# The square roots of the queries' norms, moved on the scalar engine of a decoder layer

## The chip, the core and the metric

The kernel runs on one core of a Trainium2 chip, on one NeuronCore with five engines that work side by side: TensorE (matrix products, here "PE", with "PEld" for loading its weights), VectorE ("DVE"), ScalarE ("ACT"), GpSimd ("POOL") and SyncE ("SP", which here only starts transfers). The metric is the device time of one execution in microseconds (us). The kernel before took 1009.03 us, the median of three runs (1007.69 to 1009.83).

## What is computed

A decoder layer on x of 16 x 64 x 512: self attention along one axis, cross attention to a context, and a mixture of 16 experts of which each row takes 4. The change lies in the cross attention, cut here to what matters:

```
q = (hidden @ Wq.T)  -> 32 heads of 128;   k, v -> 8 heads of 128, each used by 4 query heads
q = q * rsqrt(mean(q*q) + 1e-5) * q_norm_w          # one root for each row and head
k = k * rsqrt(mean(k*k) + 1e-5) * k_norm_w
probs = softmax(q @ k.T / sqrt(128) + mask)          # exponentials
out = (probs @ v) @ Wo.T
```

Everything is float32. The queries' norm needs a square root, the softmax an exponential. On this chip both are functions of ScalarE, and they lie in different tables: each change from one to the other shows in the trace as an instruction of its own, ACT_TABLE_LOAD. Squares and copies need no such load in this trace.

## The kernel before

The rows stand in 8 tiles of 128, taken in pairs u = 0 to 3. A head group g = 0 to 7 is one key head with its four query heads. One **step** (g, u) is one head group and one pair. `cross` runs over the steps, first g = 0 to 3 and then 4 and 5, with u inside; for the last two head groups it runs over u with (6, u) and (7, u) inside. So there are 32 steps. Around a step's own attention it does other work:

- `step_queries` (L492) normalises the queries of the step: `normed_queries` multiplies each half by its reciprocal root (L480, VectorE), turns it on TensorE (L483) and copies it out of PSUM times the weight (L489 on ScalarE or L487 on VectorE). L497 ties the two halves together.
- `attended` (L553) of the step before multiplies the turned probabilities by the values (L559) and copies the result, `at`, out (L565, ScalarE); `left_sums` (L229 to L232) makes sums of it on GpSimd, or on VectorE for the last two head groups.
- `softmaxed` (L500) makes the scores (L509), takes them out of PSUM with the mask (L514), then the maximum (L528), the difference (L529), the exponential (L530, ScalarE), the sum (L531), its reciprocal (L539) and the product (L540). For g of 6 and 7 eight shorter exponentials take the place of one (L536). L522 multiplies the next step's reciprocal roots by a one that is made from this step's scores: it changes no value and only makes them wait for the scores.
- `queries` (L447) makes the raw queries of the step three ahead, or of (7, u) in step (6, u): 28 matrix products (`seven`, L255, Strassen's scheme in Winograd's form), sums on VectorE (L459 to L463), and eight squares with their sums on ScalarE (L467). After some of them `inverse_root` takes the root (L443) and its reciprocal (L444, VectorE): for head groups 1 to 6 once for two pairs, after u = 1 and u = 3, for the last head group after every pair.
- `projected` (L573) multiplies the attention's result of the step before by Wo, again in 28 products (L255), with its sums on VectorE (L580 to L587). `right_sums` (L236 to L239) prepares the weights of a head group on GpSimd when a new one begins.
- `turned_rows` (L543) turns the probabilities (L546, TensorE) and copies them out of PSUM as `pt` (L550, ScalarE). `pt` is read by the next `attended`; its PSUM bank is one of two that all transposes share.

In the last two head groups `summed`, `normed_pair` (with a root of its own, through the same L443) and `routed_pair` follow, which prepare the experts' part. L823 enters rows into tables with indirect transfers from GpSimd.

The order on each engine is not written out by hand. It comes from the program's builder, which takes the text's order as a priority. So the order in the trace differs from the text's at places: L458, a copy that `queries` starts with, runs ahead of the exponential of `softmaxed`, which stands before it in the text.

Of the kernel before, what the change touches and what calls it, by code (L numbers as in the profile page):

```python
# [23 lines left out]
F32 = mybir.dt.float32  # L24
I32 = mybir.dt.int32
AF = mybir.ActivationFunctionType
ALU = mybir.AluOpType
AX = mybir.AxisListType

P = 128  # L30
N, C, L = 16, 64, 512
NT = N * C // P
DC = L // P
KVH, GRP, HD = 8, 4, 128
# [5 lines left out]
EPS = 1e-5  # L40
# [9 lines left out]
def decoder_layer(  # L50
# [25 lines left out]
    V, S, T, G = nc.vector, nc.scalar, nc.tensor, nc.gpsimd  # L76
# [3 lines left out]
    small = ctx.enter_context(tc.tile_pool(name="small", bufs=4))  # L80
# [13 lines left out]
    def tr_bank():  # L94
        return bank("tr", 2)

    def sc_bank():
        return bank("sc", 3)
# [90 lines left out]
    eps_sb = const.tile([P, 1], F32, tag="eps", name="eps_sb")  # L189
# [44 lines left out]
    def right_sums(engine, t, w):  # L234
        b11, b12, b21, b22 = (w[:, 2 * k : 2 * k + 2, 256 * n : 256 * n + 256] for k in range(2) for n in range(2))
        engine.tensor_sub(t[:, 0], b12, b11)  # L236
        engine.tensor_sub(t[:, 1], b22, t[:, 0])  # L237
        engine.tensor_sub(t[:, 2], b21, t[:, 1])  # L238
        engine.tensor_sub(b12, b22, b12)  # L239

    def seven(a11, a12, d, a22, s, t, w, sums_last=False):

        b11, t3, b21, b22 = (w[:, 2 * k : 2 * k + 2, 256 * n : 256 * n + 256] for k in range(2) for n in range(2))
        x, p, r = (mm_bank().rearrange("p (a n) -> p a n", a=2) for _ in range(3))
        p7 = sc_bank()[:, :256]
        products = [
            (x[:, 0], a11, b11), (x[:, 1], s[:, 1], t[:, 1]), (p7, d, t3),
            (p[:, 0], a12, b21), (p[:, 1], s[:, 2], b22),
            (r[:, 0], a22, t[:, 2]), (r[:, 1], s[:, 0], t[:, 0]),
        ]  # L250
        if sums_last:
            products = [products[k] for k in (0, 3, 5, 6, 1, 2, 4)]
        for dst, left, right in products:
            for k in range(2):
                T.matmul(dst, left[:, k, :], right[:, k, :], start=k == 0, stop=k == 1)  # L255
        return x, p7, p, r
# [173 lines left out]
    q_raw, q_ss, q_rs = {}, {}, {}  # L430
# [7 lines left out]
        left_sums(V, s, *xn_quarters(u))  # L438
        xn_sums.append(s)

    def inverse_root(x, shape, scale):
        rs = small.tile(shape, F32, tag="rs{}".format(len(shape) * shape[1]), name="rs", bufs=2)
        S.activation(rs, x, AF.Sqrt, bias=eps_sb, scale=scale)  # L443
        V.reciprocal(rs, rs)  # L444
        return rs

    def queries(g, u):  # L447
        w = wq_tiles[g]
        if u == 0:
            q_ss[g] = small.tile([P, NT, GRP], F32, tag="qss", name="qss", bufs=2)  # L450
            if g > 0:
                right_sums(G, wq_t, w)
        raws = [work.tile([P, GRP, HD], F32, tag="qraw", name="qraw", bufs=8) for _ in range(2)]
        c1, c2 = (raw.rearrange("p (a h) d -> p a (h d)", a=2) for raw in raws)
        x, p7, p, r = seven(*xn_quarters(u), xn_sums[u], wq_t, w, sums_last=(g, u) == (0, 0))
        su = work.tile([P, 2, 256], F32, tag="su", name="su", bufs=1)
        u3 = work.tile([P, 256], F32, tag="u3", name="u3", bufs=1)
        S.copy(su[:, 0], x[:, 0])  # L458
        V.tensor_add(su[:, 1], x[:, 1], su[:, 0])  # L459
        V.tensor_add(u3, p7, su[:, 1])  # L460
        V.tensor_add(c1, p, su)  # L461
        V.tensor_add(c2, r, u3.unsqueeze(1).to_broadcast([P, 2, 256]))
        V.tensor_add(c1[:, 1], r[:, 1], c1[:, 1])  # L463
        for j, raw in enumerate(raws):
            for h in range(GRP):
                square = work.tile([P, HD], F32, tag="square", name="square", bufs=1)
                S.activation(square, raw[:, h, :], AF.Square, accum_out=q_ss[g][:, 2 * u + j, h : h + 1])  # L467
            q_raw[g, 2 * u + j] = raw

        done = (0, 1, 2, 3) if g == KVH - 1 else (0, 1, 3) if g == 0 else (1, 3)  # L470
        if u in done:
            first = max([k + 1 for k in done if k < u], default=0)
            span = 2 * (u + 1 - first)
            rs = inverse_root(q_ss[g][:, 2 * first : 2 * u + 2, :], [P, span, GRP], 1.0 / HD)
            for k in range(first, u + 1):
                q_rs[g, k] = rs[:, 2 * (k - first) : 2 * (k - first) + 2, :]

    def normed_queries(g, i, on_vector):
        raw = q_raw.pop((g, i))
# [20 lines left out]
    def softmaxed(g, u, qts):  # L500
        sp = sc_bank()
        for hp in range(2):
            for b in range(2):
                for j, qt in enumerate(qts):
                    k0 = (2 * u + j) * P + b * C
                    at = ((j * 2 + hp) * 2 + b) * C

                    for h in range(2):
                        T.matmul(  # L509
                            sp[h * C : (h + 1) * C, at : at + C], qt[:, b, 2 * hp + h, :],  # L510
                            kT[g // 4][:, g % 4, k0 : k0 + C], start=True, stop=True,
                        )
        pr = work.tile([P, 8, C], F32, tag="prob", name="prob")
        V.scalar_tensor_tensor(  # L514
            pr, sp.rearrange("p (a k) -> p a k", a=8), HD**-0.5,
            mask_sb.unsqueeze(1).to_broadcast([P, 8, C]), ALU.mult, ALU.add,
        )
        after = divmod(NT // 2 * g + u + 1, NT // 2)
        if after[0] < KVH - 2:

            rs = q_rs[after]
            V.scalar_tensor_tensor(  # L522
                rs, pr[:, 0:1, 0:1].to_broadcast([P, 2, GRP]), HIGHEST, rs, ALU.is_le, ALU.mult
            )
        mx = small.tile([P, 8], F32, tag="mx", name="mx")
        sm = small.tile([P, 8], F32, tag="sm", name="sm")
        if g < KVH - 2:
            V.tensor_reduce(mx, pr, AX.X, ALU.max)  # L528
            V.tensor_sub(pr, pr, mx.unsqueeze(2).to_broadcast([P, 8, C]))  # L529
            S.activation(pr, pr, AF.Exp)  # L530
            V.tensor_reduce(sm, pr, AX.X, ALU.add)  # L531
        else:

            V.tensor_reduce(mx, pr, AX.X, ALU.max, negate=True)
            for a in range(8):
                S.activation(  # L536
                    pr[:, a, :], pr[:, a, :], AF.Exp, bias=mx[:, a : a + 1], accum_out=sm[:, a : a + 1]
                )
        V.reciprocal(sm, sm)  # L539
        V.tensor_mul(pr, pr, sm.unsqueeze(2).to_broadcast([P, 8, C]))  # L540
        return pr

    def turned_rows(pr):  # L543
        tp = tr_bank()
        for a in range(4):
            T.transpose(  # L546
                tp[:, a * P : (a + 1) * P], pr[:, 2 * a : 2 * a + 2, :], ident
            )
        pt = work.tile([P, 2, 2 * P], F32, tag="pt", name="pt", bufs=1)
        S.copy(pt.rearrange("p j t -> p (j t)"), tp)  # L550
        return pt
# [59 lines left out]
    def cross(steps):  # L611
        mixing = None
        for g, u in steps:
            if u == 1 and g + 2 < KVH:
                load_wq(g + 2)
            if u == 0 and g + 1 < KVH:
                load_wo(g + 1)
            qts = step_queries(g, u)
            if mixing:
                late.append((*mixing[:2], *attended(*mixing)))  # L620
                mixing = None
            pr = softmaxed(g, u, qts)
            if g < KVH - 2:
                queries(*divmod(NT // 2 * g + u + 3, NT // 2))
            elif g == KVH - 2:
                queries(g + 1, u)
            if (g, u) == (KVH - 3, NT // 2 - 1):
                queries(g + 1, u)
            if late:
                projected(*late.pop())  # L630
            if (g, u) == (KVH - 1, NT // 2 - 1):
                shared_hidden(0, 0, mm_bank)
            pt = turned_rows(pr)
            if g < KVH - 2 and (g, u) != steps[-1]:

                mixing = (g, u, pt)
            else:
                late.append((g, u, *attended(g, u, pt)))
            if g == KVH - 2 and u > 0:
                summed(u - 1)  # L640
                normed_pair(u - 1)
                if u > 1:
                    entered(u - 2, 1)
            if g == KVH - 1 and u > 0:
                routed_pair(u - 1)
                entered(u - 1, 0)
            if (g, u) == (KVH - 2, 0):
                load_shared(0)
            if (g, u) == (KVH - 2, NT // 2 - 1):
                load_shared(1)  # L650
# [483 lines left out]
```

## Time and profile before

| | |
|---|---|
| median of three runs | 1009.03 us (1007.69 to 1009.83) |
| the profiled execution | 1009.14 us, of which the profile's span is 1007.4 us |
| ACT_TABLE_LOAD | 18 at L443, 13 at L530, 5 at L536, each 1283 ns |
| roots of queries (L443) | 13 of 128x16 (307 ns), 6 of 128x8 (301 ns) |
| squares (L467) | 256 of 309 ns, each with a read of its sum of 187 ns |
| exponentials | 24 of 630 ns (L530), 64 of 334 ns (L536) |
| steps of the cross attention | from 192 to 730 us of the span |
| granted TensorE clock over the span | 0.990 |

How to read it: times in a view are microseconds from the start of the span. "A <- B" in a list of waits means that engine and instruction A stood idle until B was done. In the order of time each line gives the start, the length, the engine, the source line, and what is written from what; a bracket at the end gives the idle time before it and what ended it. A line of stretches gives the busy time of PE, PEld, DVE, ACT and POOL (each with a count of instructions), then the clock that TensorE was granted as a share of the full one, then the share of the DMA engines and GB/s.

### The profile page before, as it was taken

The numbers are of one execution on the slowest core, as the hardware profiler recorded it, in microseconds if no ns is written. First come the engines' busy times: TensorE is split into PE (matmuls) and PEld (weight loads), VectorE is DVE, ScalarE is ACT, GpSimd is POOL, SyncE is SP. The second block draws the span as 40 slices with busy tenths as digits, with TensorE's granted clock in tenths as the row PEclk, the third lists the DMA queues.
The fourth block names the chain that finished last, engine by engine and source line by source line (L and its number), as shares of the span: only waits on it lengthen the run. The fifth ranks groups of instructions, "written<-read, shape, count | busy, mean of one in ns | idle before, by whom it ended". The sixth has DMA issues, their size and how long they took to land. (4 is left out here: it accounts for less than half of the span.)

```text
span 1007.4 us, 14841 instructions
## 1 busy us (share of the span) xinstructions
PE 956.2 (95%) x5080; PEld 662.8 (66%) x5080; DVE 552.4 (55%) x1188; ACT 445.0 (44%) x1260; POOL 336.3 (33%) x356
## 2 busy tenths in 40 slices
PE   9999998999999999999999999988999999999994
PEld 4456555888888888887888877766754445445442
DVE  3665657876767677667767667668475111111110
ACT  2366672655454554435544675564530222222221
POOL 2131102341614427135243241033053344454433
PEclk9999999999999999999999999998999999999997
DMA  9220014200201102012020110000033966655763
GB/s 231 75 95 21 11 32 108 102 1 1 84 1 42 43 1 85 1 60 77 1 85 1 43 43 1 23 22 22 22 104 131 353 156 150 153 107 127 190 174 72
DMA packets 28960, 76.88 MB, mean 76 GB/s; under 512 B 4624, under 2 KB 9024, under 8 KB 26832
## 3 DMA queue, kind: packets, MB, share of 16 engines
q1 hardware_dynamic: 18160, 52.96, 15.8%
q0 software_dynamic: 10432, 22.66, 11.0%
q8 instruction: 42, 0.69, 0.3%
q14 instruction: 38, 0.31, 0.1%
q10 hardware_dynamic: 288, 0.26, 0.1%
HBM read 102.31 MB, written 14.97 MB: 116 GB/s over the span
## 5 line engine op out<-in xcount | busy, mean ns | idle before, releaser
L997 PE MATMUL sc<-w,xt 128*128 128x512 f32 x288 | 130.3, 593 | 2.3 <-DMA w<-in_wu_dram 2.3
L467 ACT ACTIVATE square<-qraw 128x128 f32<-128x128 f32 x256 | 79.2, 309 | 85.0 <-DVE qraw L461 42.1
L997 PEld LDWEIGHTS sc<-w,xt 128*128 128x128 f32 x288 | 51.8, 190 | 54.1 <-issue 52.4
L229 POOL TENSOR_TENSOR sat<-at 128x256 f32<-128x256 f32 x24 | 17.5, 728 | 202.2 <-ACT at L565 202.2
L1002 DVE TENSOR_TENSOR z<-sc,z 128x256 f32<-128x256 f32 x36 | 15.3, 425 | 124.8 <-ACT z L1001 118.9
L255 PE MATMUL mm<-wo_sb,at 128*128 128x256 f32 x256 | 68.8, 394 | 5.4 <-ACT at L565 5.4
L255 PE MATMUL mm<-wq_sb,xnT 128*128 128x256 f32 x256 | 72.5, 389 | 0.0
L1025 POOL DMA_INDIRECT out_dram<-y,idx x36 | 57.3, 1593 | 36.9 <-DMA out_dram<-y,idx 30.4
L1017 PE MATMUL mm<-w,zt 128*128 128x512 f32 x144 | 68.0, 594 | 1.5 <-DVE zt L1010 1.5
L255 PE MATMUL mm<-wq_t,xns 128*128 128x256 f32 x256 | 66.2, 381 | 2.6 <-POOL wq_t L237 1.5
L255 PE MATMUL mm<-wo_t,sat 128*128 128x256 f32 x256 | 67.3, 383 | 0.6 <-DVE sat L230 0.6
L979 POOL DMA_INDIRECT xg<-rows_d,idx x40 | 39.7, 993 | 75.3 <-PE tr L1008 50.5
L823 POOL DMA_INDIRECT table_d<-entry_sb,at_slot x24 | 25.6, 1065 | 111.6 <-DVE at_slot L790 105.2
L1001 ACT ACTIVATE z<-sc 128x256 f32<-128x256 f32 x36 | 13.8, 384 | 106.9 <-PE sc L997 106.9
L255 PEld LDWEIGHTS mm<-wo_sb,at 128*128 128x128 f32 x256 | 49.6, 196 | 14.4 <-ACT at L565 7.6
L255 PEld LDWEIGHTS mm<-wq_t,xns 128*128 128x128 f32 x256 | 48.3, 190 | 9.8 <-POOL wq_t L237 1.9
L255 PEld LDWEIGHTS mm<-wo_t,sat 128*128 128x128 f32 x256 | 48.7, 193 | 7.8 <-POOL wo_t L238 0.7
L1017 PEld LDWEIGHTS mm<-w,zt 128*128 128x128 f32 x144 | 27.1, 190 | 35.3 <-issue 32.1
L565 ACT COPY at<-sc 128x512 f32<-128x512 f32 x64 | 34.3, 588 | 35.3 <-PE sc L559 35.0
L480 DVE TENSOR_TENSOR qraw<-qraw,rs 128x512 f32<-128x512 f32 x64 | 48.2, 757 | 0.2
L255 PEld LDWEIGHTS mm<-wq_sb,xnT 128*128 128x128 f32 x256 | 44.3, 190 | 5.7 <-DVE su L459 0.3
L467 ACT ACTIVATION_READ_ACCUMULATOR square<-qraw 128x1 f32 x256 | 47.8, 187 | 0.0
(286 smaller groups left out, 2082.5 us busy)
## 6 DMA issues: line engine op xcount, KB each, us to landing
w<-in_wg_dram SPq DMA_DIRECT2D x40, 512.0 KB
w<-in_wu_dram SPq DMA_DIRECT2D x40, 512.0 KB
w<-in_wd_dram SPq DMA_DIRECT2D x40, 512.0 KB
wq_sb<-in_wq_dram SPq DMA_DIRECT2D x8, 1024.0 KB
wo_sb<-in_wo_dram SPq DMA_DIRECT2D x8, 1024.0 KB
xs<-in_x_dram SPq DMA_DIRECT2D x8, 256.0 KB
wv_sb<-in_wv_dram SPq DMA_DIRECT2D x2, 1024.0 KB
ct<-in_ctxt_dram SPq DMA_DIRECT2D x8, 256.0 KB
```

Of the source, the lines that this page charges most:

```text
L229: engine.tensor_add(s[:, 0], a21, a22)
L255: T.matmul(dst, left[:, k, :], right[:, k, :], start=k == 0, stop=k == 1)
L467: S.activation(square, raw[:, h, :], AF.Square, accum_out=q_ss[g][:, 2 * u + j, h : h + 1])
L480: V.tensor_mul(raw, raw, q_rs[g, i // 2][:, i % 2, :].unsqueeze(2).to_broadcast([P, GRP, HD]))
L565: S.copy(at[:, :, b * C : (b + 1) * C], pv[b].rearrange("p (a q) -> p a q", a=2 * GRP))
L823: G.indirect_dma_start(tables_d[q], bass.IndirectOffsetOnAxis(at_slots[u][:, q : q + 1], axis=0), entry_sb[:, 2 * u + j, k, :], None,)
L979: G.indirect_dma_start(xg, None, rows_d, bass.IndirectOffsetOnAxis(idx[:, b : b + 1], axis=0))
L997: T.matmul(hp, xt[:, d, :], w1_tiles[buffer(j)][:, :, d, :], start=(d == 0), stop=(d == DC - 1))
L1001: S.activation(z, hp[:, :FI], AF.Silu)
L1002: V.tensor_mul(z, hp[:, FI:], z)
L1017: T.matmul(op, zt[:, c, :], w2_tiles[buffer(j)][:, c, :], start=(c == 0), stop=(c == FI // P - 1))
L1025: G.indirect_dma_start(out, bass.IndirectOffsetOnAxis(idx[:, b : b + 1], axis=0), y, None, bounds_check=NT * P - 1, oob_is_err=False, comp ...
```

## The change

Only the place of the queries' roots changes. `queries` no longer takes them at its end, except for the first two pairs of head group 0, which are needed before the first step; it puts the task into a list, `waiting`. A new function, `query_roots`, does what stood there. It is called at two places:

- in `softmaxed` of the next step, right behind the exponential. This takes the roots of all head groups but the last.
- in `cross`, right behind `turned_rows` of the same step, for the last head group.

At both places the root's bias, the constant 1e-5, is made anew by a small instruction on VectorE from one column of the tile that the exponential, or the copy of `pt`, has just written: the minimum with 0 and then the maximum with 1e-5. Its value is always 1e-5, but the root can't start before that tile is written. The tie L522 is left out in the steps at which the next step's roots are not yet taken.

```diff
-    def inverse_root(x, shape, scale):
+    def inverse_root(x, shape, scale, eps=eps_sb):
...
-        S.activation(rs, x, AF.Sqrt, bias=eps_sb, scale=scale)
+        S.activation(rs, x, AF.Sqrt, bias=eps, scale=scale)
...
         if u in done:
             first = max([k + 1 for k in done if k < u], default=0)
-            span = 2 * (u + 1 - first)
-            rs = inverse_root(q_ss[g][:, 2 * first : 2 * u + 2, :], [P, span, GRP], 1.0 / HD)
-            for k in range(first, u + 1):
-                q_rs[g, k] = rs[:, 2 * (k - first) : 2 * (k - first) + 2, :]
+            if g == 0 and u < NT // 2 - 1:
+                query_roots(g, first, u)
+            else:
+                waiting.append((g, first, u))
+
+    waiting = []
+
+    def query_roots(g, first, u, after=None):
+        eps = eps_sb
+        if after is not None:
+
+            eps = small.tile([P, 1], F32, tag="eps", name="eps", bufs=1)
+            V.tensor_scalar(eps, after, 0.0, EPS, ALU.min, ALU.max)
+        span = 2 * (u + 1 - first)
+        rs = inverse_root(q_ss[g][:, 2 * first : 2 * u + 2, :], [P, span, GRP], 1.0 / HD, eps)
+        for k in range(first, u + 1):
+            q_rs[g, k] = rs[:, 2 * (k - first) : 2 * (k - first) + 2, :]
...
-        if after[0] < KVH - 2:
+        if after in q_rs and after[0] < KVH - 2:
...
+        while waiting:
+            query_roots(*waiting.pop(), after=pr[:, 0, 0:1])
         V.reciprocal(sm, sm)
...
             pt = turned_rows(pr)
+            if waiting and waiting[0][0] == KVH - 1:
+                query_roots(*waiting.pop(), after=pt[:, 0, 0:1])
```

## The prediction

> **What bounds the kernel.** I read the page's first part, then the list of waits for TensorE alone, then the order of time on each engine around every root (L443), then the granted clock in short stretches.
>
> ```profile
> PE 956.2 (95%) x5080; PEld 662.8 (66%) x5080; DVE 552.4 (55%) x1188; ACT 445.0 (44%) x1260; POOL 336.3 (33%) x356
> ...
> PE sc L509 <- DVE qt L497: 5.6, 7, 1.4
> PE mm L255 <- ACT at L565: 5.4, 7, 1.2
> PE sc L559 <- ACT pt L550: 4.8, 3, 2.1
> PE tr L483 <- ACT pt L550: 2.6, 5, 1.4
> ```
>
> TensorE is the bound, so the change can win only what TensorE waits for. The first line is the page's, the others are the four longest of TensorE's waits (us in total, times, longest): 18.4 us, all in the attention steps. I number the 32 steps (g,u) in order of execution; 24 to 31 are (6,0), (7,0), (6,1), (7,1) and so on. From one L509 to the next, most steps of heads 1 to 5 take 15.90 us with TensorE never idle: with a root or without one, nothing can be won there. The stalls sit in steps 1, 4, 8, 12, 16, 20, 22 and 24 to 30.
>
> In step 28 the order of time (start, length) on ScalarE, then on TensorE, and a row of the stretches read:
>
> ```profile
> 661.50 1.28 ACT L443 ACT_TABLE_LOAD   x1
> 662.79 0.30 ACT L443 ACTIVATE rs<-qss,eps_sb 128x8 f32<-128x8 f32 x1
> 663.00 0.56 ACT L550 COPY pt<-tr 128x512 f32<-128x512 f32 x1
> 664.78 1.07 ACT L565 COPY at<-sc 128x512 f32<-128x512 f32 x2 [1.22 <-PE sc L559]
> ...
> 663.62 1.14 PE L559 MATMUL sc<-pt,v 64*128 64x256 f32 x8 [2.06 <-ACT pt L550]
> ...
> 666.00:667.00 1.00, 1.00 (x3) 0.82 (x4) 1.00 (x5) 0.05 (x1) 0.99 (x1) 0.50 0.03 1
> ```
>
> The load and the root stand ahead of pt, whose transposes ended at 661.55; TensorE waits 2.06 us, then 1.16 us for `at`. After that its granted clock (third number from the right) is 0.50 from 666.0 to 669.4. Step 30 is the same (2.06, 1.16, half clock from 700.1 to 706.9).
>
> **The change, part by part.**
>
> *Counts.* All 23 roots stay (19 of queries, 4 of L668). Of 18 loads for the root and 13 for L530 one each goes, as steps 23 and 24 no longer switch twice. Of 23 ties (L522, 240 ns) 11 go; 17 `eps` instructions on VectorE come, a 128x1 tensor_scalar, which the rows of L720 and L723 give at 0.15 us: 2.6 us out, 2.6 in. No DMA is moved, and nothing passes SP's or POOL's queue.
>
> *The new place, heads 0 to 5.* The load needs no operand, so it runs right behind the exponential; the root then needs `eps`. In step 4 the exponential and what follows it on ScalarE:
>
> ```profile
> 255.93 0.63 ACT L530 ACTIVATE prob<-prob 128x512 f32<-128x512 f32 x1 [1.43 <-DVE prob L529]
> 258.72 0.31 ACT L467 ACTIVATE square<-qraw 128x128 f32<-128x128 f32 x1 [2.16 <-DVE qraw L461]
> ```
>
> Load and root are 1.28 + 0.31 = 1.59 us; the gap behind an exponential without a load before it is 2.16 us, so they are covered. The load back (1.28) falls before the next step's exponential, as now, in its 1.43. Behind the root wait the squares on ScalarE, then on VectorE the reciprocal and two L480, which the transposes need only some 7 us later. If the cover were gone, squares would move pt, which waits 1.34 us on its own in step 5: a slip under that costs nothing. Cost taken: 0; bounds 0 and 0.5 us in each of 12 steps (VectorE holding L463 beyond the 1.76 us that it ends ahead of the product needing its bank: 277.81 against 279.57).
>
> *Step 1.* The load at 205.23 holds the `at` copies; TensorE's 0.42 goes: **-0.4**.
>
> *Steps 4, 8, 12, 20.* pt is 0.50 us late, TensorE waits 0.29; then L497 takes 0.81 instead of 0.18 us and the next scores wait (step 4, POOL and VectorE):
>
> ```profile
> 267.10 1.27 POOL L239 TENSOR_TENSOR wo_sb<-wo_sb 128x512 f32<-128x512 f32 x1
> 267.59 0.81 DVE L497 SCALAR_TENSOR_TENSOR qt<-qt 128x8 f32<-128x8 f32 x1
> ```
>
> L497 is held until POOL's L239 is nearly over. With pt on time, L497 would start 2.82 us behind L546's start, as in step 6 (281.30 to 284.12): at 267.10, the very hundredth in which L239 starts. Ahead of it, the step is 15.90 instead of 17.02: 1.1 us won; behind it, it ends where it does now: 0. Among near ties of 0.01 or 0.02 us in this trace (L522 against L230) VectorE lost two and won two. Half: 4 x 1.1 / 2, **-2.2** (0 to -4.4).
>
> *Step 16.* pt could start at 459.70, not 461.31. L483 then comes 1.55 us earlier, L497 at 461.92 ends with POOL's L237 near 462.2 instead of 464.62; of that 2.4 I take **-2.0** (-1.4 to -2.4).
>
> *Step 22.* The reciprocal of head group 6, which has no tie, lets four L480 (2.65 us) in ahead of L487 and L497; the step is 17.21. These move behind step 23's exponential, where VectorE idles 0.8 to 1.1 us three times: **-1.3** (0 to -1.3).
>
> *Steps 24 and 25.* The roots of (6,2) and (6,3) come behind eight exponentials: squares 1.6 us later, ending at 597.0, still ahead of pt (598.26). But the root of (7,0) comes behind pt, so its first L480 goes from 597.35 to about 600, among POOL's eight operations of right_sums, and each operation that alternates with them waits up to 1.3 us. TensorE's 0.36 before the projection becomes 1.2, and the sums of `at` finish later: **+1.5** (0 to +3).
>
> *Step 26.* pt was on time; now load and root (to 629.1) hold the `at` copies, 628.80 before: **+0.3**.
>
> *Steps 28 and 30.* pt starts at 661.56, L559 at 662.2; its `at` copies could start 1.16 later, but load and root end at 663.64. The projection starts at 664.76, not 665.90: -1.1. With 0.67 + 1.5 us of stalls around 1.13 of work, instead of 2.06 + 1.16, half clock becomes unlikely: in step 26 (0.68 + 1.16) it stayed at 1.00. Half clock for 3.4 us costs 1.7 us; VectorE, busy without a break from 656 to 667.7, lets 1.3 of it through: **-2.4** (0 to -2.8). Step 30 gains more, as L559 itself took 2.08 at half clock: -1.1 and -1.9, **-3.0** (0 to -3.6).
>
> The halving in rows comes with gaps of 2.06 us at most. [...]
>
> The load's row is 1.28 us and the root starts 1.29 behind it (263.91, 265.20). [...]
>
> **Sum.** -0.4 - 2.2 - 2.0 - 1.3 + 1.5 + 0.3 - 2.4 - 3.0 = -9.5. The profiled execution took 1009.14 (span 1007.4 and 1.74 around it), 0.11 above the median of the runs. Forecast: **999.6 us**. It reaches the end because the stages behind stay TensorE's (711 to 770: busy 57.16 of 59).
>
> **Rivals.**
> - *Half clock stays* in 28 and 30, as the new stall of 1.5 us keeps the stretch thin: +3.2, 1002.8. For it: 1.13 of work in 3.3 us. Against it: step 26.
> - *The gain is eaten in heads 0 to 5*: VectorE takes `eps`, then waits for the root in order, and L461 to L463 slip past their 1.76 us: 12 x 0.6 = +7.2, 1006.8. For it: VectorE waits up to 2.1 us for a root today (L444). Against it: the engines' order already differs with and without a load, so the load is reckoned with in it.
> - *Slower: the queries of (7,u) become the wait.* Behind pt now stand load, root, reciprocal, L480, transposes, L489: 1.28 + 0.31 + 0.2 + 0.69 + 0.65 + 0.69 = 3.8, less 1.13 of L559: 2.7 us for each of four steps, if TensorE has the transposes L483 ahead of the projection. +10.7, against the gains outside of 24 to 30 (5.9) and half a stall: about 1013. It decides once more than two of the four steps are so ordered. For it: step 24 has that order. Against it: in 26, 28 and 30 L483 comes some 8 us behind L559.
>
> **Chances.** Forecast 0.55 (its own range 996 to 1003), half clock 0.17, eaten 0.15, slower 0.13. A measurement of this kernel tells about 0.2% (2 us) from no change. Faster: 0.55 + 0.17 + half of the third = 0.79; same 0.10; slower 0.11. The range reaches from all ties won and little lost in 24, 995.5, to the third case, 1007.
>
> **What would show it.** Loads of L443 17, of L530 12; the load right behind L530 in steps 1, 3, ... 23; "L559 <- pt" and "L483 <- pt" nearly gone from TensorE's waits; L497 at 0.18 in about half of steps 4, 8, 12, 20; clock 1.00 through steps 28 and 30; step 25 longer. Wrong if the written order isn't kept on the engines: already L458 runs ahead of the exponential that the text puts before it.

## The result, and the profile after

The changed kernel takes **1002.1 us** (median of four runs, 1000.3 to 1002.5) against 1009.0: a ratio of 0.993, 95% interval 0.991 to 0.995. The forecast was 999.6 with a range of 995.5 to 1007.0. The gain is 6.9 us where 9.5 were expected. The profiled execution took 1002.03 us, with a span of 1000.3.

TensorE's row of the page and its longest waits in the attention steps after the change (L487, L497, L509, L546, L550, L559 and L565 are now L500, L510, L522, L561, L565, L574 and L580; L480 and L483 are L493 and L496):

```profile
PE 953.4 (95%) x5080; PEld 661.5 (66%) x5080; DVE 549.3 (55%) x1194; ACT 441.7 (44%) x1258; POOL 334.7 (33%) x356
```

```profile
PE mm L255 <- ACT at L580: 5.9, 6, 1.4
PE sc L522 <- DVE qt L510: 4.3, 5, 1.2
...
PE sc L574 <- ACT pt L565: 2.0, 3, 0.7
...
PE tr L496 <- DVE qraw L493: 1.7, 2, 1.0
```

Of the two waits for `pt` (4.8 and 2.6 us) 2.0 are left. The wait for `at` has grown by 0.5 us, the one for the tie has shrunk by 1.3 us, and one is new: transposes that wait for the queries of the last head group (L493). The loads stand as counted, in the groups of ScalarE by line (busy us, ns of one, then its idle time before):

```profile
L443 ACT ACT_TABLE_LOAD x17 | 21.8, 1283 | 10.3 <-DVE eps L485 10.2
L543 ACT ACT_TABLE_LOAD x12 | 15.4, 1283 | 0.2
```

The 10.2 us of idle time in the first line are no part of the forecast. In step 9 the exponential, the load and the root read:

```profile
334.49 0.63 ACT L543 ACTIVATE prob<-prob 128x512 f32<-128x512 f32 x1 [0.84 <-DVE prob L542]
336.05 1.28 ACT L443 ACT_TABLE_LOAD   x1 [0.93 <-DVE eps L485]
337.35 0.31 ACT L443 ACTIVATE rs<-qss,eps 128x16 f32<-128x16 f32 x1
```

The load did not run right behind the exponential but stood 0.93 us until `eps` was written, and so in eleven of the twelve steps (3, 5, ... 23). In steps 26, 28 and 30 it starts 0.02 us behind the copy of `pt`, as was forecast.

The difference by steps, each from its first scores to the next step's, the last one to the first product of the shared expert (L868 before, L885 after):

| steps | before, us | after, us | difference | forecast |
|---|---|---|---|---|
| 1 | 13.77 | 13.31 | -0.46 | -0.4 |
| 4, 8, 12, 20 | 68.06 | 66.92 | -1.14 | -2.2 |
| 16 | 17.29 | 14.86 | -2.43 | -2.0 |
| 22 | 17.21 | 15.89 | -1.32 | -1.3 |
| 24 and 25 | 30.47 | 34.01 | +3.54 | +1.5 |
| 26 and 27 | 36.39 | 36.39 | 0.00 | +0.3 |
| 28 and 29 | 37.05 | 34.69 | -2.36 | -2.4 |
| 30 and 31 | 26.58 | 23.28 | -3.30 | -3.0 |

All other steps are equal to 0.02 us. The sum is -7.47. The steps also begin 0.99 us earlier (192.45, 191.46), ahead of anything that was changed, and what follows them takes 1.33 us more: from 717.97 to 721.38, shortly behind the last L574, the clock is halved, and the last product with the gate (L753) ends 1.69 us later behind the shared expert's first one than before. That makes 7.1 us of span.

So two terms missed, the ties and steps 24 and 25. Step 24 on TensorE (start, length; the bracket is the idle time before and what ended it), and the stretches around it (busy PE, PEld, DVE, ACT, POOL, then the granted clock):

```profile
591.54 0.60 PE L561 MATMUL tr<-ident,prob 128*128 128x128 f32 x4
592.82 1.14 PE L574 MATMUL sc<-pt,v 64*128 64x256 f32 x8 [0.67 <-ACT pt L565]
595.00 1.07 PE L496 MATMUL tr<-ident,qraw 128*128 128x128 f32 x4 [1.04 <-DVE qraw L493]
596.76 1.09 PE L496 MATMUL tr<-ident,qraw 128*128 128x128 f32 x4 [0.70 <-DVE qraw L493]
```

```profile
591.60:595.00 3.40, 1.68 (x14) 1.00 (x12) 2.60 (x6) 1.85 (x4) 3.13 (x3) 1.00 0.71 289
595.20:598.40 3.20, 2.50 (x10) 1.71 (x9) 3.17 (x3) 1.20 (x2) 3.20 (x3) 0.50 0.00 0
598.60:601.80 3.20, 3.20 (x35) 2.38 (x34) 3.20 (x3) 1.27 (x1) 3.12 (x3) 0.50 0.00 0
```

The four transposes take 1.07 instead of 0.66 us: TensorE ran at half clock here for 6.8 us, which it did not before. In steps 28 and 30 the half clock of before is gone.

### The profile page after: what moved, and what is told of

Its sections match the earlier page's. It is cut to its first block, busy times and chain, and to the rows that moved or that the text cites. A ratio compares the mean times of both kernels' runs of the same rounds, so it can differ in the third digit from the quotient of the medians.

```text
span 1000.3 us, 14858 instructions
## 1 busy us (share of the span) xinstructions
PE 953.4 (95%) x5080; PEld 661.5 (66%) x5080; DVE 549.3 (55%) x1194; ACT 441.7 (44%) x1258; POOL 334.7 (33%) x356
## 5 line engine op out<-in xcount | busy, mean ns | idle before, releaser
L467 ACT ACTIVATE square<-qraw 128x128 f32<-128x128 f32 x256 | 79.0, 308 | 65.7 <-DVE qraw L463 38.7
L580 ACT COPY at<-sc 128x512 f32<-128x512 f32 x64 | 34.3, 587 | 31.7 <-PE sc L574 31.4
L493 DVE TENSOR_TENSOR qraw<-qraw,rs 128x512 f32<-128x512 f32 x64 | 47.8, 753 | 0.5
L467 ACT ACTIVATION_READ_ACCUMULATOR square<-qraw 128x1 f32 x256 | 47.7, 186 | 0.0
```

The source lines that it names most:

```text
L493: V.tensor_mul(raw, raw, q_rs[g, i // 2][:, i % 2, :].unsqueeze(2).to_broadcast([P, GRP, HD]))
L580: S.copy(at[:, :, b * C : (b + 1) * C], pv[b].rearrange("p (a q) -> p a q", a=2 * GRP))
```

## The experiments

Theory: the parts of the change act one by one, and each term of the table has the cause that the prediction named. Rivals: the two misses come from another part of the change than was thought, or the half clock follows something else than TensorE's idle time. The lengths of steps below are read from each run's trace; the medians stand beside the kernel before on the same chip, which took 1009.2 to 1009.8 us there.

**The two halves apart.** The roots of the last head group back in the queries:

```diff
-            if g == 0 and u < NT // 2 - 1:
+            if (g == 0 and u < NT // 2 - 1) or g == KVH - 1:
```

> The changed kernel, but the roots of head group 7 are taken in the queries again, ahead of the copy of the turned probabilities; the roots of heads 1 to 6 stay behind the exponential. My theory: the two halves of the change add up. Steps 1, 4, 16 and 22 keep what they gained (0.5 + 1.1 + 2.4 + 1.3 = 5.3 us), steps 24 and 25 take 30.5 us again instead of 34.0, and steps 28 and 30 fall back to their old lengths, half clock included (37.05 for 28 and 29, 22.5 for 30): 1009.0 - 5.3 = 1003.7 us. Rival: the loss in steps 24 and 25 comes from the roots of (6,2) and (6,3), which stand behind the eight exponentials here too, so they stay at 34.0 us and the time is 1007.2.

Measured: 1006.7 us, ratio 0.997 (0.995 to 0.999), 3 us above the expectation. Steps 1, 16 and 22 kept their gains to 0.02 us. Step 4 lost its tie here (17.01), so all four ties were lost. Steps 24 and 25 took 31.17 us: neither number of the expectation, but most of the loss is gone, and 0.70 us stay with the exponential's half. Steps 28 and 29 took 37.69, 30 and 31 28.12, each with one more stretch of half clock than before.

The other half alone:

```diff
-            if g == 0 and u < NT // 2 - 1:
+            if g < KVH - 1:
```

> The kernel before, but with the roots of head group 7 behind the copy of the turned probabilities; heads 0 to 6 as before. My theory: steps 28 and 30 gain 2.4 + 2.0, steps 24 and 25 lose 3.5, and nothing else moves: 1009.0 - 0.9 = 1008.1 us. Rival (steps 24 and 25 lose only by both halves together): they lose 0 to 1 us here and the time is 1004.6 to 1005.6.

Measured: 1010.9 us, ratio 0.9995 (0.997 to 1.002): nothing won. Steps 28 and 29 (34.70) and 30 and 31 (23.28) are those of the changed kernel, but steps 24 and 25 took 36.73 us, worse than in both cases expected. The load is not shared with the roots of (6,2) and (6,3) any more, so it stands between `pt` and the root, and TensorE waits 2.27 us for L493, with 10.2 us of half clock behind it. The two halves help each other here.

**The root of (7,0) alone**, ahead of `pt` again:

```diff
-            if g == 0 and u < NT // 2 - 1:
+            if (g == 0 and u < NT // 2 - 1) or (g, u) == (KVH - 1, 0):
```

> The changed kernel, but the root of (7,0), the first of the last head group, is taken in the queries, ahead of the copy of the turned probabilities; those of (7,1) to (7,3) stay behind it. My theory: the 3.5 us lost in steps 24 and 25 come from this one root being late, so that its L493 meet POOL's sums and the clock is halved. Here steps 24 and 25 take 30.5 us (30.2 to 31.0), the clock is 1.00 in them, and the time is 1002.1 - 3.5 = 998.6 us. Rival: another part of the change (the squares 1.6 us later, the roots of (6,2) and (6,3) behind eight exponentials) is the cause: 33 to 34 us for the two steps, 1001.1 to 1002.1 in all.

Measured: 1000.8 us, ratio 0.991 (0.990 to 0.993); steps 24 and 25 take 31.16 us at a clock of 1.00 (30.2 to 31.0 were expected, and 998.6 us in all). So 2.85 of the 3.54 us belong to this one root, as the theory has it. The other 0.70 are in the first experiment too. VectorE's order in step 24 of this run:

```profile
592.44 0.68 DVE L493 TENSOR_TENSOR qraw<-qraw,rs 128x512 f32<-128x512 f32 x1
593.04 0.20 DVE L444 RECIPROCAL rs<-rs 128x8 f32<-128x8 f32 x1
593.15 0.69 DVE L602 TENSOR_TENSOR acc<-mm,acc 128x512 f32<-128x512 f32 x1
593.76 2.93 DVE L493 TENSOR_TENSOR qraw<-qraw,rs 128x512 f32<-128x512 f32 x2
```

The first line is the last of four L493 of (6,2) and (6,3), whose roots now come behind step 24's exponentials; before, all four (L480) ran from 581.17 to 584.27, ahead of step 24. Now they fill VectorE until the reciprocal that (7,0) needs, and TensorE takes L574 first and waits 0.68 us for `pt`, where before it had a transpose of (7,0) to do. The last line shows that the two L493 of (7,0) meet POOL's sums in this run too: 2.93 us, where the two L480 took 0.69 and 1.16 before, and TensorE waits 0.89 us for the second. That the order and this meeting make the 0.70 us is read from the trace; no run tried either by itself.

**Clock or wait.** Two runs fill stalls of TensorE with matmuls whose results nobody reads, without making anything else earlier. In the kernel before, five of them ahead of L559 in steps 28 and 30:

```diff
         pv = [sc_bank() for _ in range(2)]
+        for _ in range(5 if g == KVH - 2 and u >= 2 else 0):
+            T.matmul(
+                pv[0][:, :256], v[g // 4][:C, 2 * u, g % 4 * HD : (g % 4 + 1) * HD],
+                last["pr"][:C, :4, :], start=True, stop=True,
+            )
```

> The kernel before, with five matmuls of 64x256 more in steps 28 and 30, between the transposes of the probabilities and L559, written to the bank that L559 then overwrites; they need nothing that L559 waits for, and fill 1.4 of TensorE's 2.06 us there. All else is unchanged, the late copy too. My theory: the clock goes by the idle share of a fixed stretch of 3.41 us (in the traces so far it fell behind stretches with 1.72 us of idle time or more and stayed at 1.00 up to 1.69), so it stays at 1.00 in steps 28 and 30; 28 and 29 take some 35.8 instead of 37.05 us, step 30 some 20.6 to 21 instead of 22.46, and the time is 1009.0 - 3 = 1006 us. Rival: the clock answers to something else (the load of the root's table, VectorE being busy): half clock as before, 1009.

Measured: 1005.0 us, ratio 0.995 (0.993 to 0.996). The stretches of step 28 in this run:

```profile
659.00:662.00 3.00, 2.37 (x13) 1.69 (x12) 3.00 (x9) 2.86 (x11) 2.39 (x3) 1.00 0.02 1
662.00:665.50 3.50, 2.34 (x16) 1.68 (x15) 3.50 (x9) 2.24 (x6) 2.58 (x4) 1.00 0.01 1
665.50:669.00 3.50, 3.50 (x19) 2.91 (x20) 2.32 (x8) 1.80 (x3) 2.09 (x2) 1.00 0.07 18
```

`pt` is as late as before (2.07 us behind the transposes), the load is where it was, and the clock stays at 1.00. Steps 28 and 29 take 35.43 us, 30 and 31 24.23. The half clock's price is thus 1.62 and 2.35 us; the change's earlier `pt` adds 0.74 and 0.95 to that (to 34.69 and 23.28).

In the changed kernel, step 24 alone, two ahead of L574 as above and three behind it, which read `pt` and write to a bank of the transposes:

```diff
+        if (g, u) == (KVH - 2, 0):
+            spare = tr_bank()
+            for _ in range(3):
+                T.matmul(
+                    spare[:, :256], v[g // 4][:C, 2 * u, g % 4 * HD : (g % 4 + 1) * HD], pt[:C, 0, :],
+                    start=True, stop=True,
+                )
```

> The changed kernel, with five matmuls of 64x256 more in step 24 alone: two between the transposes of the probabilities and L574 (0.56 us in a stall of 0.67), three behind L574 (0.84 us in a stall of 1.04), results unused. My theory: of the 2.85 us that the late root of (7,0) costs in steps 24 and 25 (34.01 against 31.17 with the root early), the larger part is half clock, 6.8 us of it. With the stalls filled the clock stays at 1.00 and the two steps take 32.0 us (31.7 to 32.6); the time is 1002.1 - 2 = 1000 us. Rival: the loss is the late L493 and their meeting with POOL alone, the half clock runs beside VectorE's sums: 33.5 to 34.2 us for the two steps, 1002 in all.

Measured: steps 24 and 25 take 32.48 us at full clock, so 1.53 us of the loss were half clock. The time is 1001.9 us, ratio 0.992 (0.990 to 0.994), and not 1000: in this execution half clock fell into step 30 instead (24.75 against 23.28 us). That led to a count of all traces (last section).

**The tie.** Steps 8, 12 and 20 of the changed kernel are still long, for one hundredth of a microsecond. VectorE in step 4, which was won, and in step 8, then POOL in the same two:

```profile
265.66 0.18 DVE L510 SCALAR_TENSOR_TENSOR qt<-qt 128x8 f32<-128x8 f32 x1
...
329.25 1.28 DVE L510 SCALAR_TENSOR_TENSOR qt<-qt 128x8 f32<-128x8 f32 x1
```

```profile
265.67 1.32 POOL L239 TENSOR_TENSOR wo_sb<-wo_sb 128x512 f32<-128x512 f32 x1
...
329.24 1.26 POOL L239 TENSOR_TENSOR wo_sb<-wo_sb 128x512 f32<-128x512 f32 x1
```

In step 4 the tie starts 0.01 us ahead of L239 and takes 0.18 us, in step 8 it starts 0.01 behind and takes 1.28. The edit makes the tie read its first operand from the bank of PSUM (`turned`, which `normed_queries` returns as well) that the second tile is copied from:

```diff
-            first, second = (qt[:, :, :, 0:1] for qt in qts)
+            first = qts[0][0][:, :, :, 0:1]
+            second = qts[1][1].rearrange("p h b q -> p b h q")[:, :, :, 0:1]
             V.scalar_tensor_tensor(first, second, HIGHEST, first, ALU.is_le, ALU.mult)
```

> The changed kernel, but the tie of the two query tiles (L510, 128x8) reads its first operand from the bank of PSUM that the second tile was copied from, not from the second tile in SBUF; same size, same wait, same place. My theory: in steps 8, 12 and 20 the tie is held by POOL's L239 since both read two operands from SBUF; with one operand in PSUM it takes 0.25 us or less beside POOL, those steps take 15.90 instead of 17.01 us, and the time is 1002.1 - 3.3 = 998.8 us (step 16 may give 0.2 more). Rival: VectorE and POOL exclude one another whatever the operand, or those steps are long for another reason: they stay at 17.0 us and the time at 1002.1.

Measured: **995.5 us**, ratio 0.986 (0.984 to 0.988), twice what was expected. Step 8 on VectorE, and POOL beside it:

```profile
326.56 0.75 DVE L500 TENSOR_SCALAR qt<-tr,qw_sb 128x512 f32<-128x512 f32 x1 [1.08 <-PE tr L496]
327.23 0.16 DVE L511 SCALAR_TENSOR_TENSOR qt<-tr,qt 128x8 f32<-128x8 f32 x1
```

```profile
326.19 1.27 POOL L237 TENSOR_TENSOR wo_t<-wo_sb,wo_t 128x512 f32<-128x512 f32 x1
327.42 1.27 POOL L239 TENSOR_TENSOR wo_sb<-wo_sb 128x512 f32<-128x512 f32 x1
```

It takes 0.158 to 0.162 us in all 24 steps, POOL busy or not. With both inputs in SBUF it took 1.28 us in steps 8, 12 and 20 of the changed kernel and in step 8 ended 0.03 us behind POOL's L239 (330.54, 330.51); with one in PSUM it takes 0.16 us inside POOL's L237 (326.19 to 327.46). So in these steps POOL held the tie with both inputs in SBUF and not with one, as expected; what POOL reads was not varied. The unexpected part: the unhindered steps are shorter by 0.13 us too (15.77 instead of 15.90). The old tie, which read the result of L500, started 0.85 us behind L500's start (328.40 to 329.25), behind its end; the new one 0.67. That this dependence is the cause is read from these times and was not tested by itself. Only steps 15 and 16 together lost, by 0.29 us.

The same edit on the kernel before:

> The kernel before, with nothing changed but the tie's first operand, taken from PSUM. My theory: the tie's meeting with POOL is a matter of its two operands in SBUF, not of when the late copy lets it start, so it goes here as well: every step of heads 0 to 5 is 0.13 us shorter, steps 4, 8, 12 and 20 keep only TensorE's own 0.29 us of the late copy and take 16.06 instead of 17.02 us, 24 x 0.13 + 4 x 0.83 = 6.4 us in all: 1002.6 us. The change is then worth 1002.6 - 995.5 = 7 us on top of it, through other steps. Rival: without the change's earlier copy the tie still ends late in those steps (17.0 us): 1006.

Measured: 1003.9 us, ratio 0.995 (0.993 to 0.997). Steps 4, 8, 12 and 20 take 16.26 (16.06 expected), the others 15.77, but step 16 grew to 17.81, so from step 1 to the shared expert 5.4 us are won and not 6.4. The change on top of it is worth 7.0 us over the same stretch (503.65 to 496.68), as it is without it (7.5). The tie's cost was therefore for the most part not in the change's value; it lay beside it. Half a microsecond between single executions is no more than the half clock of one stretch, which falls in them by chance (last section).

**The cover in heads 0 to 5.** Four more squares on ScalarE, which stand ahead of the root in the text:

```diff
         span = 2 * (u + 1 - first)
+        for _ in range(4 if after is not None and g < KVH - 2 else 0):
+            square = work.tile([P, HD], F32, tag="square", name="square", bufs=1)
+            S.activation(square, q_raw[g, 2 * u][:, 0, :], AF.Square, bias=eps)
```

> The changed kernel, with four squares of 128x128 more on ScalarE (about 1.2 us, result unused) between the load and the root in each of the 12 steps of heads 0 to 5 that take one: load, squares and root are then 2.8 us against a gap of 2.16 us behind the exponential. My theory: the slip of 0.6 us is taken up by the 1.34 us that ScalarE waits for the transposes later, and VectorE's sums still end ahead of the product that needs their bank: the steps stay at 15.90 us (17.01 where the tie is late). Rival: VectorE, which waits in order for the root, holds the sums beyond that and TensorE waits 0.5 us or more in each of the 12 steps: 6 us in all, 1008.

Measured (one run): 1000.3 us. The order on ScalarE is not the one that was meant. Step 9 of this run:

```profile
338.33 0.40 ACT L489 ACTIVATE square<-qraw,eps 128x128 f32<-128x128 f32 x1 [0.95 <-DVE eps L485]
338.75 1.28 ACT L443 ACT_TABLE_LOAD   x1
340.04 0.31 ACT L443 ACTIVATE rs<-qss,eps 128x16 f32<-128x16 f32 x1
340.26 1.25 ACT L489 ACTIVATE square<-qraw,eps 128x128 f32<-128x128 f32 x3
```

One square stands ahead of the load, three stand behind the root. The root starts 3.29 us behind the start of the exponential (336.75), against 2.86 in the changed kernel: 0.4 us later and not 1.2. The squares of L467 behind it come 1.7 us later. Step 23 has no squares more, as its root is that of head group 6, so eleven steps were tried. Ten are unchanged, with the order on VectorE somewhat altered; step 1 grew by 1.07 us, where TensorE now waits for `pt`. So 1.7 us more work on ScalarE at the new place costs nothing, except in step 1; a root that is 1.2 us later was not tried. A by-product: with no half clock in this execution, steps 24 and 25 took 32.25 us, near the 32.48 with the stalls filled.

**A better version.** The PSUM tie and the early root of (7,0) together:

> The changed kernel with both edits that helped: the tie's first operand from PSUM, and the root of (7,0) ahead of the copy of the turned probabilities. My theory: they add up. Steps 1 to 23 as with the tie alone (15.77 us), steps 24 and 25 at 31.1 us instead of 33.25: 2.1 us less than with the tie alone, ratio to the kernel before 0.984, 993 us. Rival: with the tie changed the steps are shifted so that the early root gains nothing: 0.986, 995 us.

Measured: **992.7 us**, ratio 0.983 (0.981 to 0.985). Steps 24 and 25 take 31.16 us; the parts add up.

With two matmuls more in the stall behind L574, `u >= 2` in the first run and `u >= 1` in the second (the edit of step 24 above, with `g == KVH - 2` and `range(2)`):

> As the run with both edits, and two matmuls of 64x256 more behind L574 in steps 28 and 30 (0.56 us in a stall of 1.43), results unused. My theory: the stalls of those steps (0.6 + 0.7 + 1.4 us) trip the half clock only where the fixed stretch of 3.41 us takes in over 1.7 us of them, which it did in step 30 in two of four runs of this form, for 1.5 us. With 0.56 us filled it doesn't any more: 0 to 1.5 us less than with both edits alone, 0.7 in the mean; a ratio of 0.983. Rival: the matmuls stand in the way of the projection and cost 0.3 us or more.

> As the run with both edits and the two matmuls more, but these in step 26 too, where the half clock fell in the last run of this form (23.63 us instead of 22.37). My theory: with 0.56 us of each stall of 1.43 filled, no stretch of 3.41 us in steps 26, 28 and 30 has over 1.7 us of idle time, so the clock is 1.00 through them (22.4, 20.5, 20.5 us) in every execution, and the time is at most that of both edits alone, 0 to 2 us below it: 991 us, ratio 0.982. Rival: the clock falls as before, now here, now there, and nothing is won: 0.983 or above.

Measured: 991.2 us, ratio 0.983 (0.980 to 0.985), and 993.1 us, ratio 0.984 (0.981 to 0.986). In the first the clock was 1.00 in steps 28 and 30, but fell in step 26 (1.26 us); in the second it was 1.00 from step 24 to 30, as expected. No gain in time over both edits alone can be told from that: the intervals overlap, and the half clock behind the last L574 came in both. In the second run the rival's ratio, 0.983 or above, is what was measured.

## Why the prediction was nearly right

- **What bounds**: right. All that was won came from stalls of TensorE; where it had none and no tie, the steps are equal to 0.02 us. But "never idle" was not exact: in the steps of 15.90 us TensorE is busy for 15.84, and with the tie from PSUM they take 15.77, so something could be won there by another change.
- **The new place in heads 0 to 5, at nothing**: right in what it cost, wrong in how. The load waited for `eps`, so load and root ended 2.53 us behind the exponential in eleven steps, not 1.59, and that is more than the gap of 2.16 us that was to cover them. The slip cost nothing all the same, and in ten steps 1.7 us more work on ScalarE cost nothing either. Where it is taken up, in the 1.34 us that `pt` waits or on VectorE, no run shows. The rival that the gain is eaten there fell.
- **Step 1, 22 and 16**: right, -0.46, -1.32 and -2.43 (the -2.0 was taken inside a bound of 2.4).
- **Steps 4, 8, 12 and 20**: the mechanism was right, to the hundredth (L510 at 329.25, L239 at 329.24), the size was not: one tie of four was won, not two, -1.14 for -2.2. In the five traces with this tie and the earlier copy in heads 0 to 5 (the changed kernel, the exponential's half alone, the early root, the filled stalls, the four squares more) it is one of twenty. The four near ties of L522 against L230 that gave the even chance were another pair of instructions.
- **Steps 24 and 25**: the step that failed. Late root, L493 among POOL's sums: both came, and cost 1.1 to 1.3 us (32.25 and 32.48 without half clock against 31.16 with the root early). The four L493 of (6,2) and (6,3), by the order in the trace, add most or all of 0.70 more: the step had followed the squares of this move on ScalarE, not its products on VectorE. That is 1.8 to 2.0 for a forecast of 1.5. What the term lacked above all is the half clock, 1.53 us. The prediction looked for it only where it was to vanish, and not where its own new stalls (0.67 + 1.04 us in the 3.4 us ahead of the fall at 595.09) were dense enough.
- **Steps 28 and 30**: right in sum, -5.66 for -5.4, and nearly so in parts: half clock 1.62 and 2.35 (1.3 and 1.9 expected), earlier projection 0.74 and 0.95 (1.1 each). Most of what looked like the price of a late copy was the clock's.
- **The rival that half clock stays** was half true: never in step 28 of the seven executions with the change's late root and no filling, but in step 30 of four, at 1.47 us each. The changed kernel's own profiled execution was one of the three without it.
- **The slower rival**, queries of (7,u) as the wait, came in step 24 alone, for the reason given (its transposes stand ahead of the projection). In 26, 28 and 30 they do not, and the load behind `pt` costs nothing there beyond what `at` waits.
- **The sum**: the two misses are 1.06 and 2.04 us; steps 16, 26 and 30 gave 1.0 us more than their terms and so made up a third of them. The 0.99 us ahead of the steps and the 1.33 us behind them were in no term, and they nearly cancel by luck.

## What to carry to other kernels

Before work is moved, add up TensorE's idle time in each 3.4 us around its old and its new place: a stall that let the clock fall cost 1.3 to 2.4 us on top of its length here, and the new stalls of step 24 (0.67 + 1.04 us in such a stretch) cost it again, 1.53 us. Where a small instruction of VectorE decides a step, look at what POOL does beside it and whether an operand can come from PSUM; that was worth 5.4 to 6.6 us here, about as much as the whole change. Look at the wait ahead of a table load as well: here a root that waits for a late operand got its load no earlier in eleven steps of twelve (0.93 us of idle time ahead of it in step 9). And follow a moved root to all that needs it, on every engine: what went wrong in step 24 was on VectorE and TensorE, not on the engine that was relieved.

## What the runs showed of the hardware

**In the attention steps the clock fell behind fixed stretches with 1.70 us of idle time or more.** In each trace the times at which the granted clock falls and rises lie on one grid of 3.41 us, whose phase differs from execution to execution (falls at 665.96 us before and at 595.09 in the changed kernel, 20.8 stretches apart). In all thirteen traces, laid on their own grids, every stretch at full clock between 190 and 705 us with 1.70 us of TensorE idle time or more (15 of them, up to 2.28) was followed by half clock, and none with 1.69 or less (the highest 1.69, 1.67, 1.62): about half of the stretch. Two stretches in step 30 of two runs, by the trace of the run with both edits and then of the changed kernel:

```profile
684.73:688.13 3.40, 1.53 (x10) 1.06 (x11) 3.24 (x9) 2.93 (x5) 2.66 (x3) 1.00 0.05 6
688.20:691.50 3.30, 3.30 (x10) 2.56 (x9) 2.80 (x10) 0.76 (x2) 2.69 (x3) 0.50 0.03 3
```

```profile
690.70:694.00 3.30, 2.14 (x12) 1.40 (x10) 3.26 (x8) 3.03 (x15) 2.60 (x3) 1.00 0.05 6
694.10:697.40 3.30, 1.82 (x11) 1.32 (x12) 3.28 (x9) 2.54 (x4) 2.63 (x3) 1.00 0.02 1
```

The stalls are the same, 2.8 us in all; in the first the grid puts 1.88 of them into one stretch, in the second it cuts them into 1.2 and 1.5. So the same step gains or loses 1.5 us by chance there.

What stays open: behind the last L574 half clock came in six of the traces (from 717.97 in the changed kernel) after stretches with only 0.1 to 0.9 us of idle time, and once ahead of the cross attention (at 159 us, in the first of the two runs with the matmuls more) after 1.4 us. The six stretches hold 8 to 18 matmuls of 128x16. Counted as idle, these would bring them to 2.0 to 2.3 us; but other stretches that come to 1.8 us in this way were not followed by half clock, so such a matmul would have to count for a part. No run tested that. The runs also say nothing of why POOL wins most of the ties.
